# Layer 0's score rows in a four-layer graph network: broadcast transposes on TensorE, or one transpose and a trip through DRAM

## The chip, the cores and the metric

The kernel runs on one core of a Trainium2 chip. The metric is the device time of one execution in microseconds; lower is better. Five engines work side by side, each with its own queue of instructions: TensorE (PE) multiplies, VectorE (DVE) and ScalarE (ACT) do the elementwise work, GpSimd (POOL) does little here, and SyncE (SP) issues every DMA of the kernel's loop.

## The reference

32 graphs of 512 nodes with 256 features go through four layers. Each layer is followed by a residual sum and a layernorm. What matters here is layer 0, an attention with four heads of 64 features over the graph's edges:

```python
h = jnp.einsum('bnd,hde->bhne', nodes_embed, W)
e_src = jnp.einsum('bhne,hte->bhtn', h, a_src)
e_dst = jnp.einsum('bhne,hte->bhtn', h, a_dst)
...
    weight = weight + mask * (e_src[:, :, t, :, None] + e_dst[:, :, t, None, :])
weight = jax.nn.leaky_relu(weight, negative_slope=0.01)
weight = jnp.where(node_adj[:, None] == 0, NEG, weight)
attention = jax.nn.softmax(weight, axis=-1)
dst = jnp.einsum('bhij,bhje->bhie', attention, h) + bias[None, :, None, :]
out = jax.nn.relu(dst) + h
```

The score of an edge from i to j is a number of node i plus a number of node j. Layers 1 and 3 are attentions of the same kind with one head, layer 2 is a transformer block (eight heads and a feed forward).

## The kernel before

Each graph is held as four tiles of 128 nodes (R = 4) by 256 features (two halves, K = 2), all in float32. A matmul in float32 appears in the profile as two instructions; a transpose appears as one.

**Score rows.** The kernel lays the scores out with the key node j on the partitions and the query node i along the row. A leaky relu of a sum, exponentiated, is a maximum of products, so one VectorE instruction makes a tile of unnormalised attention: `kept` (line 393) takes `gb`, which is exp of the query's number, the same row of 512 on all 128 partitions, and `ex`, one number for each partition, and computes max(gb, ex) * edges. To get `gb`, `along` takes a column of 128 numbers for each node tile, repeats it 128 times, and transposes that on TensorE (four transposes of 128 by 128 into one PSUM bank, tile `gp`). ScalarE copies the bank to SBUF (line 345). Layer 0 calls `along` once for each of its four heads; layers 1 and 3 once each.

**Names.** h0p, h1p and h3p are the projections of layers 0, 1 and 3; o0, o1 and o3 here stand for their attention products, which the profile lists as `o<-hv,pt` (layer 0) and `o<-h,pt` (layers 1 and 3). hv is layer 0's value matrix. xt1p, xt2p, xt3p and ytp are transposes of a layer's input, ctp those of layer 2's context, qkp and vp the projections of layer 2, s its scores, cp its attention product, wop its output projection, f1p and f2p its feed forward.

**Order of work.** The function `graph` is a generator that does one small chunk of work at a time and then yields a key, `PERIOD * b + PLACES[name][i]`, where b is the graph. `heapq.merge` runs the chunks of all 32 graphs by their keys. PERIOD is 12054, and a graph's keys go from -1440 to 42379, so that some four graphs are under way at any time. In the TensorE queue the instructions stand in exactly this order (`manual_schedule`); in the other queues (DVE, ACT, POOL, SP) the framework orders them when the program is built, by what it estimates to be ready. [...]

**Buffers.** Tags are shared inside stages: layers 0 and 1 are stage a, layer 2's attention stage b, feed forward and layer 3 stage c. In stage a there are seven buffers of the tag `part`, which holds `kept`'s tiles, two for `gb`, and two PSUM banks. The adjacency halves (`adjt` for the mask at lines 363 and 371, `adj` for layer 2's symmetric mask at lines 384 to 387) all go through one buffer, so each load (line 351) waits in SP's queue until the half before it has been used up. Layer 2's scores of the last of four key tiles are masked by a matmul on TensorE in both kernels.

Of the kernel before, what the change touches and what calls it, by code (L numbers as in the profile page):

```python
# [9 lines left out]
F32 = mybir.dt.float32  # L10
# [10 lines left out]


F32R = mybir.dt.float32r
SHUT = -(2.0**127)


PERIOD = 12054
PLACES = {
    "edges": [-1440, -1440, -410, 1420],
    "x": [3260],  # L30
    "mask": [16220, 16520, 16600, 17520],
    "layer 0": [
        2410, 3594, 4534, 4534, 5073, 5753, 5753, 5823, 6123, 6123, 6233, 6233, 6603, 6773, 6903,
        7687, 7687, 7777, 8077, 8077, 8157, 8287, 8439, 8439,
    ],
    "layer 1": [11037, 11066, 11277, 11729, 11849, 11879, 12043, 13286, 13554, 14195, 14884],
    "qkv": [17180, 17740, 18270, 18270, 18270, 18990, 19484, 19654, 21635, 21635],
    "attention": [
        20262, 20932, 21922, 21982, 22092, 22092, 22092, 22350, 22350, 23077, 23537, 23537,
        24028, 24208, 24328, 24532, 25064, 25220, 25368, 25943,  # L40
    ],
    "projection": [26801, 26801, 26861, 26911, 27661, 27721, 28721, 29140, 29256, 29848],
    "feed forward": [
        31013, 31120, 32042, 32263, 32263, 32465, 32710, 33771, 33983, 34076, 34284, 34691,
        35070, 35329, 35615, 36103, 36646, 37299,
    ],
    "layer 3": [39714, 39714, 40906, 41226, 41406, 41526, 41526, 42359, 42359, 42379, 42379],
}
STAGES = {"edges": "a", "x": "a", "layer 0": "a", "layer 1": "a", "feed forward": "c", "layer 3": "c"}
ALL = mybir.DependencyInfo(mybir.DependencyClass.Sync, mybir.DependencyReason.DATA)  # L50
# [22 lines left out]
def fast_path(ctx: ExitStack, tc: tile.TileContext, a: dict, out: bass.AP, bad: bass.AP):  # L73
# [8 lines left out]
    nc = tc.nc  # L82
    B, N, D = a["x"].shape
    P = 128
    R = N // P
    K = D // P
    H, _, HO = a["w0"].shape
# [13 lines left out]
    def product(what, *args, **kwargs):  # L101
        latest[0] = what(*args, **kwargs).ins.name  # L102
# [19 lines left out]
    ident = const.tile([P, P], F32, name="ident")  # L122
# [24 lines left out]
    cols = const.tile([P, 5 * K + NF], F32, name="cols")  # L147
# [89 lines left out]

    sb = ctx.enter_context(tc.tile_pool(name="sb", bufs=1))  # L240
    ps = ctx.enter_context(tc.tile_pool(name="ps", bufs=2, space=bass.MemoryType.PSUM))
    stage = ["a"]

    def buf(shape, tag, name, bufs, dtype=F32):

        return sb.tile(shape, dtype, tag=tag + stage[0], name=name, bufs=bufs)

    def bank(name, dtype=F32):
        shape = [P, 2048 // (2 if dtype == BF16 else 4)]
        n = 4 if stage[0] == "b" else 2  # L250
        return ps.tile(shape, dtype, tag="mm" + stage[0], name=name, bufs=n)

    def part(name):

        return buf([P, N], "part", name, {"a": 7, "b": 6, "c": 5}[stage[0]])

    def all_rows(v):
        return v.unsqueeze(1).to_broadcast([P, R, D])

    def layernorm(y, eps):  # L260

        st = buf([P, R, 6], "bn", "bn", 2)
        mv = buf([P, R, 2], "mv", "mv", 2)
        rs = buf([P, 3, R], "rs", "rs", 2)
        for r in range(R):
            nc.vector.bn_stats(st[:, r, :], y[:, r, :])  # L266
            nc.vector.bn_aggr(mv[:, r, :], st[:, r, :])
        var = mv[:, :, 1]
        nc.vector.scalar_tensor_tensor(rs[:, 0, :], var, eps, var, op0=ALU.add, op1=ALU.max)  # L269
        nc.gpsimd.tensor_tensor(rs[:, 1, :], rs[:, 0, :], mhalf[:, :R], op=ALU.pow)  # L270
        nc.vector.scalar_tensor_tensor(  # L271
            rs[:, 2, :], mv[:, :, 0], -1.0, rs[:, 1, :], op0=ALU.mult, op1=ALU.mult
        )
        for r in range(R):
            nc.scalar.activation(  # L275
                y[:, r, :],
                y[:, r, :],
                AF.Identity,
                bias=rs[:, 2, r : r + 1],
                scale=rs[:, 1, r : r + 1],  # L280
            )
# [37 lines left out]
    def project(xt, w, cols, name):  # L319

        h = buf([P, R, cols], "h", name, {"a": 2}.get(stage[0], 1))
        for r in range(R):
            yield
            p = bank(name + "p")
            for k in range(K):
                product(nc.tensor.matmul,
                    p[:, :cols],
                    xt[:, k, r * P : (r + 1) * P],
                    w[:, k, :cols],
                    start=k == 0,  # L330
                    stop=k == K - 1,
                )
            nc.scalar.copy(h[:, r, :], p[:, :cols])
        return h

    def along(cols, name):

        yield
        p = bank("gp")
        for r in range(R):  # L340
            product(nc.tensor.transpose,
                    p[:, r * P : (r + 1) * P], cols[:, r, :].to_broadcast([P, P]), ident
            )
        g = buf([P, N], "gb", name, {"a": 2}.get(stage[0], 1))
        nc.scalar.copy(g, p)  # L345
        return g
# [27 lines left out]
    def symmetric(b, at):  # L374
# [4 lines left out]
        for h in range(2):  # L379
# [3 lines left out]
            for r in range(h * R // 2, (h + 1) * R // 2):  # L383
                in_place(nc.vector.tensor_max(parts[r], at[:, r, :], t[:, r % (R // 2), :]))
                diag = parts[r][:, r * P : (r + 1) * P]
                nc.vector.tensor_max(diag, diag, identb)
        nc.vector.tensor_scalar(shut, shut, 0.0, SHUT, op0=ALU.is_equal, op1=ALU.mult)
        return a2, shut

    def kept(name, g, edges, f):  # L390

        t = part(name)
        nc.vector.scalar_tensor_tensor(t, g, f, edges, op0=ALU.max, op1=ALU.mult)  # L393
        return t


    def layer0(x, xt, at, rd):
        h = yield from project(xt, w0, D + 2 * H, "h0")
        values = hv[:, :, :, :HO]
        nc.vector.tensor_add(  # L400
            values,
            h[:, :, :D].rearrange("p r (h e) -> p r h e", h=H),
            bias0.rearrange("p (h e) -> p h e", h=H).unsqueeze(1).to_broadcast([P, R, H, HO]),
        )
        ex = buf([P, 2, H, R], "ex", "ex0", 2)
        s, d = h[:, :, D : D + H], h[:, :, D + H :]
        nc.scalar.activation(ex[:, 0], s.rearrange("p r h -> p h r"), AF.Exp, scale=-0.99)
        nc.scalar.activation(ex[:, 1], d.rearrange("p r h -> p h r"), AF.Exp, scale=0.99)
        nc.scalar.activation(hv[:, :, :, HO], d, AF.Exp, scale=0.01)
        nc.vector.tensor_mul(values, values, hv[:, :, :, HO:].to_broadcast([P, R, H, HO]))  # L410
        y = sb.tile([P, R, D], F32, tag="y", name="y0", bufs=3)
        for hh in range(H):
            gb = yield from along(ex[:, 0, hh, :].unsqueeze(2), "gb0")
            pt = [kept("pt0", gb, at[:, j, :], ex[:, 1, hh, j : j + 1]) for j in range(R)]
            p = bank("o0")
            o = p[:, : R * HC].rearrange("p (r c) -> p r c", r=R)
            for r in range(R):
                yield
                for j in range(R):
                    product(nc.tensor.matmul,  # L420
                    o[:, r, :],
                        pt[j][:, r * P : (r + 1) * P],
                        hv[:, j, hh, :],
                        start=j == 0,
                        stop=j == R - 1,
                    )
            rdh = rd[:, hh * R : (hh + 1) * R].unsqueeze(2)
            nc.vector.reciprocal(rdh, o[:, :, HO:])  # L428
            nc.vector.scalar_tensor_tensor(
                y[:, :, hh * HO : (hh + 1) * HO],  # L430
                o[:, :, :HO],
                0.0,
                rdh.to_broadcast([P, R, HO]),
                op0=ALU.max,
                op1=ALU.mult,
            )
        nc.vector.tensor_add(x, x, all_rows(bet0))
        nc.vector.tensor_add(y, y, h[:, :, :D])
        head_layernorm(y, 1e-6)
        nc.vector.tensor_mul(y, y, all_rows(gam0))  # L440
        nc.vector.tensor_add(y, y, x)
        layernorm(y, 1e-5)
        return y
# [41 lines left out]
    def qkv(x):  # L485
        xt = yield from transposed([x[:, r, :] for r in range(R)], "xt2")
        qk = []
        for c in range(K):
            t = [sb.tile([P, 2, 2, N], F32R, tag="qk", name="qk", bufs=3) for _ in range(2)]
            for s in range(2):  # L490
# [10 lines left out]
                bias = bqk[:, s * K + c : s * K + c + 1]  # L501
                hi = sb.tile([P, N], F32R, tag="hi", name="hi", bufs=2)
                lo = sb.tile([P, N], F32R, tag="lo", name="lo", bufs=2)
                nc.scalar.activation(hi, p, AF.Identity, bias=bias)
# [155 lines left out]
    def layer3(x, at, rd):  # L660
# [16 lines left out]
        layernorm(x, 1e-5)  # L677
        return x

    ends = [0, R * H, R * (H + 1), R * (H + 1 + H2), ND]  # L680
    def load_x(b):
        xt = sb.tile([P, K, N], F32, tag="xt0", name="xt0", bufs=1)
# [63 lines left out]
            pass  # L746


    fine = sb.tile([P, 3], F32, name="fine")
    same = sb.tile([P, 2 * B], F32, name="same")  # L750
    nc.vector.tensor_tensor(same, sums[:, 0, :], sums[:, 1, :], op=ALU.is_equal)
    nc.vector.tensor_reduce(fine[:, 0:1], same, axis=X, op=ALU.min)
    nc.vector.tensor_reduce(fine[:, 1:2], ok, axis=X, op=ALU.min)
# [1 line left out]
    p = bank("badp")  # L755
# [645 lines left out]
```

## Time and profile before

| what | value |
|---|---|
| time, median of 3 runs | 3910.18 us (3910.09 to 3910.24) |
| the profiled execution's own time | 3906.41 us |
| span of its profile | 3904.6 us |
| PE busy | 3753.3 us (96% of the span) |
| DVE busy | 2674.8 us (69%) |
| ACT busy | 1926.2 us (49%) |
| DMA engines, mean busy share of queue 1 | 23.1% |

The profile's busy time of PE comes from pipelined matmuls whose ends are modelled, so that neighbouring matmuls overlap in it. What a matmul really takes from PE is read better as the distance from the start of one group in the timeline to the start of the next.

### The profile page before, as it was taken

How to read it: one execution, taken by the hardware profiler on the slowest of the kernel's cores; microseconds unless marked ns; L12 is line 12 of the kernel's file. 1: busy time of each engine (PE TensorE's matmuls, PEld its weight loads, DVE VectorE, ACT ScalarE, POOL GpSimd, SP SyncE). 2: the span in 40 equal slices, each digit the busy share in tenths (PEclk: the TensorE clock that was granted, in tenths of full speed). 3: DMA queues.
4: the chain of work that ended last, by engine and by line, in shares of the span. 5: the costliest groups of instructions: out<-in, count | busy, mean ns of one | idle time of the engine just before them, and what ended most of it. 6: DMA issues, size and time to landing. Idle time of an engine off the chain costs nothing.

```text
span 3904.6 us, 53602 instructions
## 1 busy us (share of the span) xinstructions
PE 3753.3 (96%) x19238; PEld 2824.5 (72%) x19238; DVE 2674.8 (69%) x5594; ACT 1926.2 (49%) x4257; POOL 346.9 (9%) x266
## 2 busy tenths in 40 slices
PE   5899999999999999999999999999999999999996
PEld 4577777777777777777777777777777777777764
DVE  4667676677677677677677677677777677777653
ACT  2444455444455544455544455545555544555442
POOL 0000010000010001010001010001010001010000
PEclk6899999999999999999999999999999999999998
DMA  3222222222222222222222222222222222221120
GB/s 106 77 73 65 72 58 67 71 76 67 70 60 65 71 76 69 68 62 63 71 76 71 66 63 64 69 76 71 66 65 65 65 76 74 63 67 58 49 54 12
DMA packets 180431, 261.20 MB, mean 67 GB/s; under 512 B 36800, under 2 KB 72768, under 8 KB 180160
## 3 DMA queue, kind: packets, MB, share of 16 engines
q1 hardware_dynamic: 180160, 257.71, 23.1%
q8 instruction: 155, 2.54, 0.3%
q14 instruction: 116, 0.95, 0.1%
HBM read 106.57 MB, written 16.78 MB: 32 GB/s over the span
## 4 chain that ended last, share of the span: by engine, by line
PE 60%; DVE 14%; issue 8%; ACT 5%; POOL 5%; POOLq 0%; ACTq 0%
PE o L102 16%; PE f1p L102 7%; PE f2p L102 6%; PE qkp L102 5%; PE cp L102 5%; DVE pr L556 4%; ACT y L275 4%; POOL rs L270 3%; PE h3p L102 3%; PE s L102 3%; PE h1p L102 3%; PE wop L102 3%; POOL st L297 2%; PE gp L102 2%; PE vp L102 2%
## 5 line engine op out<-in xcount | busy, mean ns | idle before, releaser
L556 DVE TENSOR_TENSOR pr<-pr,a 128x1024 f32<-128x1024 f32 x384 | 459.1, 1216 | 319.3 <-ACT pr L553 319.2
L275 ACT ACTIVATE y<-y,rs 128x256 f32<-128x256 f32 x768 | 398.4, 589 | 438.2 <-DVE rs L271 438.2
L393 DVE SCALAR_TENSOR_TENSOR pt<-gb,ex,at 128x512 f32<-128x512 f32 x768 | 530.6, 744 | 77.6 <-ACT gb L345 77.6
L553 ACT ACTIVATE pr<-s 128x512 f32<-128x512 f32 x1024 | 545.2, 613 | 7.4 <-PE s L102 7.3
L102 PEld LDWEIGHTS o<-hv,pt 128*128 128x128 f32 x4096 | 508.4, 199 | 23.7 <-issue 8.4
L102 PE MATMUL o<-hv,pt 128*128 128x65 f32 x4096 | 502.7, 280 | 9.7 <-DVE pt L393 9.7
L102 PE MATMUL f2p<-wf,ft 128*128 128x256 f32 x2048 | 491.6, 383 | 12.3 <-ACT ft L638 12.2
L102 PE MATMUL cp<-pr,v 128*64 128x512 f32 x2048 | 474.9, 600 | 17.8 <-DVE pr L556 17.1
L102 PE MATMUL f1p<-yt,wf 128*128 128x256 f32 x2048 | 488.9, 381 | 0.3 <-DVE yt L302 0.3
L102 PE MATMUL o<-h,pt 128*128 128x257 f32 x2048 | 482.8, 383 | 3.7 <-DVE pt L393 3.7
L102 PEld LDWEIGHTS o<-h,pt 128*128 128x128 f32 x2048 | 381.5, 190 | 96.0 <-issue 40.6
L270 POOL TENSOR_TENSOR rs<-rs,mhalf 128x4 f32<-128x4 f32 x192 | 246.2, 1282 | 2118.8 <-DVE rs L269 1826.0
L638 ACT ACTIVATE ft<-f1p,cols 128x256 f32<-128x256 f32 x512 | 215.2, 474 | 442.2 <-PE f1p L102 442.2
L102 PEld LDWEIGHTS f2p<-wf,ft 128*128 128x128 f32 x2048 | 380.1, 191 | 69.5 <-ACT ft L638 17.1
L102 PEld LDWEIGHTS f1p<-yt,wf 128*128 128x128 f32 x2048 | 385.3, 191 | 54.5 <-DVE yt L302 0.8
L102 PE MATMUL s<-qk 128*128 128x512 f32 x1024 | 395.1, 481 | 1.6 <-ACT pr L553 1.6
L102 PEld LDWEIGHTS cp<-pr,v 128*64 128x64 f32 x2048 | 133.0, 136 | 286.0 <-issue 194.2
L266 DVE BATCH_NORM_STATS2 bn<-y 128x6 f32<-128x256 f32 x768 | 294.6, 411 | 4.5
L102 PEld LDWEIGHTS s<-qk 128*128 128x128 f32 x1024 | 187.8, 190 | 99.3 <-issue 40.6
L102 PE MATMUL qkp<-xt,wqkv 128*128 128x512 f32 x512 | 231.3, 594 | 0.0
L345 ACT COPY gb<-gp 128x512 f32<-128x512 f32 x192 | 111.5, 581 | 219.4 <-PE gp L102 219.4
L428 DVE RECIPROCAL rd<-o 128x4 f32<-128x4 f32 x128 | 23.4, 183 | 272.7 <-PE o L102 272.7
(134 smaller groups left out, 4582.5 us busy)
## 6 DMA issues: line engine op xcount, KB each, us to landing
qk<-hi SPq DMA_DIRECT2D x1024, 64.0 KB, 2.0
qk<-lo SPq DMA_DIRECT2D x1024, 64.0 KB, 2.0
adjt<-in_adjt SPq DMA_DIRECT2D x64, 512.0 KB, 3.5
adj<-in_adj SPq DMA_DIRECT2D x64, 512.0 KB, 3.6
xt<-in_xt SPq DMA_DIRECT2D x32, 512.0 KB, 3.4
x<-in_x SPq DMA_DIRECT2D x32, 512.0 KB, 4.7
out<-y SPq DMA_DIRECT2D x32, 512.0 KB, 3.0
wf<-in_w1t SPq DMA_DIRECT2D x1, 1024.0 KB, 7.6
```

The source lines that it names most:

```text
L102: latest[0] = what(*args, **kwargs).ins.name
L266: nc.vector.bn_stats(st[:, r, :], y[:, r, :])
L270: nc.gpsimd.tensor_tensor(rs[:, 1, :], rs[:, 0, :], mhalf[:, :R], op=ALU.pow)
L275: nc.scalar.activation(y[:, r, :], y[:, r, :], AF.Identity, bias=rs[:, 2, r : r + 1], scale=rs[:, 1, r : r + 1],)
L297: nc.gpsimd.tensor_tensor(st[:, 2, :], st[:, 1, :], mhalf[:, :G], op=ALU.pow)
L345: nc.scalar.copy(g, p)
L393: nc.vector.scalar_tensor_tensor(t, g, f, edges, op0=ALU.max, op1=ALU.mult)
L428: nc.vector.reciprocal(rdh, o[:, :, HO:])
L553: nc.scalar.activation(t[:, i, :], s, AF.Exp, scale=QSCALE)
L556: nc.vector.tensor_mul(t, t, edges)
L638: nc.scalar.activation(ft[:, f, :], p[:, f, :], AF.Relu, bias=bf1[:, ff + f : ff + f + 1])
```

## The change

Layer 0 no longer calls `along`. After the two exponentials it transposes its sixteen columns (four heads by four node tiles) with one PE transpose, whose result is 16 rows of 128. ScalarE copies that to SBUF, a DMA writes it to an 8 KB tile in DRAM, and for each head another DMA reads that head's 512 numbers back onto all 128 partitions (256 KB written to SBUF). The rows of heads 0 and 1 are read at once, those of heads 2 and 3 after `kept` of heads 0 and 1. The exponential for hv and its product (lines 409 and 410) now stand after the DMAs' issue. `along` stays for layers 1 and 3. All keys in PLACES are new except for PERIOD, and two small tiles at the end of the program reuse buffers of `part`.

```diff
@@ (keys; "mask", "qkv", "attention", "projection", "feed forward" are new likewise)
-    "edges": [-1440, -1440, -410, 1420],
-    "x": [3260],
+    "edges": [-1240, -980, -470, 1660],
+    "x": [2610],
-    "mask": [16220, 16520, 16600, 17520],
+    "mask": [16880, 17050, 18310, 18310],
     "layer 0": [
-        2410, 3594, 4534, 4534, 5073, 5753, 5753, 5823, 6123, 6123, 6233, 6233, 6603, 6773, 6903,
-        7687, 7687, 7777, 8077, 8077, 8157, 8287, 8439, 8439,
+        3070, 4014, 4464, 4464, 5583, 5783, 5783, 6433, 6733, 6803, 6803, 6803, 6803, 7163, 7163,
+        7163, 7193, 9097, 9397, 9397, 9397, 9397, 9437, 9437, 9507,
     ],
-    "layer 1": [11037, 11066, 11277, 11729, 11849, 11879, 12043, 13286, 13554, 14195, 14884],
-    "qkv": [17180, 17740, 18270, 18270, 18270, 18990, 19484, 19654, 21635, 21635],
+    "layer 1": [11147, 11176, 12027, 12297, 12297, 12357, 12357, 13366, 13784, 13784, 15794],
+    "qkv": [17230, 17350, 18880, 19150, 19220, 19520, 20214, 20764, 21625, 21825],
...
-    "projection": [26801, 26801, 26861, 26911, 27661, 27721, 28721, 29140, 29256, 29848],
+    "projection": [25751, 26941, 27351, 27471, 27941, 28071, 28841, 29450, 29706, 30078],
...
-    "layer 3": [39714, 39714, 40906, 41226, 41406, 41526, 41526, 42359, 42359, 42379, 42379],
+    "layer 3": [40234, 40464, 41356, 41486, 41656, 41686, 41686, 42299, 42359, 42829, 43129],
@@
+    dram = ctx.enter_context(tc.tile_pool(name="dram", bufs=1, space=bass.MemoryType.DRAM))
@@ layer0
         nc.scalar.activation(ex[:, 1], d.rearrange("p r h -> p h r"), AF.Exp, scale=0.99)
+        rows = yield from rows_of(ex[:, 0].rearrange("p h r -> p (h r)"), "gr0")
+        gbs = []
+        for hh in range(2):
+            yield
+            gbs.append(over(rows, hh, "gb0"))
         nc.scalar.activation(hv[:, :, :, HO], d, AF.Exp, scale=0.01)
         nc.vector.tensor_mul(values, values, hv[:, :, :, HO:].to_broadcast([P, R, H, HO]))
         y = sb.tile([P, R, D], F32, tag="y", name="y0", bufs=3)
         for hh in range(H):
-            gb = yield from along(ex[:, 0, hh, :].unsqueeze(2), "gb0")
+            gb = gbs[hh]
             pt = [kept("pt0", gb, at[:, j, :], ex[:, 1, hh, j : j + 1]) for j in range(R)]
+            if hh + 2 < H:
+                yield
+                gbs.append(over(rows, hh + 2, "gb0"))
@@ new functions
+    def rows_of(cols, name):
+        m = cols.shape[1]
+        yield
+        p = bank("gp")
+        product(nc.tensor.transpose, p[:m, :P], cols, ident)
+        g = buf([m, P], "gr", name, 1)
+        nc.scalar.copy(g, p[:m, :P])
+        rows = dram.tile([m, P], F32, tag="rows", name=name + "d", bufs=2)
+        nc.sync.dma_start(rows, g)
+        return rows
+    def over(rows, i, name):
+        g = buf([P, N], "gb", name, 2)
+        src = rows[i * R : (i + 1) * R]
+        nc.sync.dma_start(g, bass.AP(tensor=src.tensor, offset=src.offset, ap=[[0, P], [1, N]]))
+        return g
@@ end of the program
-    fine = sb.tile([P, 3], F32, name="fine")
-    same = sb.tile([P, 2 * B], F32, name="same")
+    fine, same = part("fine")[:, :3], part("same")[:, : 2 * B]
```

More of the change, by code (lines that the diff above doesn't have):

```diff
@@ L28 @@
 PLACES = {
-    "edges": [-1440, -1440, -410, 1420],
-    "x": [3260],
-    "mask": [16220, 16520, 16600, 17520],
+    "edges": [-1240, -980, -470, 1660],
+    "x": [2610],
+    "mask": [16880, 17050, 18310, 18310],
     "layer 0": [
-        2410, 3594, 4534, 4534, 5073, 5753, 5753, 5823, 6123, 6123, 6233, 6233, 6603, 6773, 6903,
-        7687, 7687, 7777, 8077, 8077, 8157, 8287, 8439, 8439,
-    ],
-    "layer 1": [11037, 11066, 11277, 11729, 11849, 11879, 12043, 13286, 13554, 14195, 14884],
-    "qkv": [17180, 17740, 18270, 18270, 18270, 18990, 19484, 19654, 21635, 21635],
+        3070, 4014, 4464, 4464, 5583, 5783, 5783, 6433, 6733, 6803, 6803, 6803, 6803, 7163, 7163,
+        7163, 7193, 9097, 9397, 9397, 9397, 9397, 9437, 9437, 9507,
+    ],
+    "layer 1": [11147, 11176, 12027, 12297, 12297, 12357, 12357, 13366, 13784, 13784, 15794],
+    "qkv": [17230, 17350, 18880, 19150, 19220, 19520, 20214, 20764, 21625, 21825],
     "attention": [
-        20262, 20932, 21922, 21982, 22092, 22092, 22092, 22350, 22350, 23077, 23537, 23537,
-        24028, 24208, 24328, 24532, 25064, 25220, 25368, 25943,
+        20372, 21892, 22112, 22292, 22292, 22292, 22292, 22460, 22460, 23187, 23727, 23727,
+        24138, 24388, 24438, 25282, 25284, 25540, 25618, 26963,
     ],
-    "projection": [26801, 26801, 26861, 26911, 27661, 27721, 28721, 29140, 29256, 29848],
+    "projection": [25751, 26941, 27351, 27471, 27941, 28071, 28841, 29450, 29706, 30078],
     "feed forward": [
-        31013, 31120, 32042, 32263, 32263, 32465, 32710, 33771, 33983, 34076, 34284, 34691,
-        35070, 35329, 35615, 36103, 36646, 37299,
+        31123, 31230, 32013, 32313, 32393, 33195, 33320, 33881, 34093, 34186, 34364, 34741,
+        34820, 35365, 35395, 35883, 36226, 37209,
     ],
-    "layer 3": [39714, 39714, 40906, 41226, 41406, 41526, 41526, 42359, 42359, 42379, 42379],
+    "layer 3": [40234, 40464, 41356, 41486, 41656, 41686, 41686, 42299, 42359, 42829, 43129],
 }
```

## The prediction

> **What bounds the kernel now.** I read the page's busy times first, then one steady period in windows, then what PE waits for in it, and then the timeline of PE around layer 0. The page:
>
> ```profile
> PE 3753.3 (96%) x19238; PEld 2824.5 (72%) x19238; DVE 2674.8 (69%) x5594; ACT 1926.2 (49%) x4257; POOL 346.9 (9%) x266
> ```
>
> PE leads. The chain of work shows the same layernorm on POOL at 1898.55 and 2015.33 us, so a period (one graph in, one out) is 116.8 us. The window of that length gives busy PE, PEld, DVE, ACT, POOL, granted clock, DMA share and GB/s; PE's waits in the same window follow:
>
> ```profile
> 1898.55:2015.35 116.80, 115.11 (x602) 86.98 (x601) 83.09 (x174) 60.03 (x135) 10.78 (x9) 1.00 0.24 68
> ...
> PE gp L102 <- ACT ex L665: 0.7, 1, 0.7
> PE xt3p L102 <- ACT y L275: 0.5, 3, 0.2
> PE cp L102 <- DVE pr L556: 0.5, 1, 0.5
> ```
>
> PE is idle for 1.7 us of 116.8, in three places. The kernel is bound by PE's own work in its fixed order: what leaves PE is gained, and every microsecond for which PE waits at its next instruction is lost. Windows at 1000 and 3000 us give the same 115.11; 31 such periods are 3621 us, the rest (some 284 us) is filling and draining. Now the timeline of PE where layer 0 begins, and that of VectorE beside it (start, duration):
>
> ```profile
> 1960.22 0.60 PE L102 MATMUL gp<-ident,ex 128*128 128x128 f32 x4
> 1964.27 0.65 PE L102 MATMUL gp<-ident,ex 128*128 128x128 f32 x4 [0.70 <-ACT ex L665]
> 1966.50 3.68 PE L102 MATMUL o<-hv,pt 128*128 128x65 f32 x32
> 1970.02 0.60 PE L102 MATMUL gp<-ident,ex 128*128 128x128 f32 x4
> 1970.46 3.64 PE L102 MATMUL o<-h,pt 128*128 128x257 f32 x16
> ...
> 1963.23 2.72 DVE L393 SCALAR_TENSOR_TENSOR pt<-gb,ex,at 128x512 f32<-128x512 f32 x4
> 1967.34 2.73 DVE L393 SCALAR_TENSOR_TENSOR pt<-gb,ex,at 128x512 f32<-128x512 f32 x4
> ```
>
> Read: the transposes of head 0 start at 1960.22, its products 6.3 us later, without a wait; the group of layer 3 (1964.27) has 6.2 us until its products (1970.46). A group of four transposes takes 0.44 us from PE (1970.02 to 1970.46); starts likewise give 0.88 for one row tile of o0, 1.73 for one of o3, 0.865 for a wop chunk. The four tiles of `kept` take 2.7 us.
>
> **What the Trainium skill says.** "DMA: Bandwidth & Descriptors", section "Latency and other measured facts", puts the fixed cost of a DMA near 2 us, mostly the receipt from the target; the trace agrees (64 KB land after 2.0 us). Its section "Two DMAs through the same engine are not ordered" says that a DMA which reads what another wrote has to be held at the issuing engine until the first has completed: the two latencies add, and SP stands still in between. No DMA in this trace reads back what another wrote. The one read of exactly `over`'s form (2 KB onto 128 partitions) is in the trace three times; the row of the one that went alone at 48.55 us, and the usual small one:
>
> ```profile
> a<-in_a SPq DMA_DIRECT2D x1, 256.0 KB, 3.1
> ...
> qk<-hi SPq DMA_DIRECT2D x1024, 64.0 KB, 2.0
> ```
>
> Beside two half-megabyte loads it took 5.8 us.
>
> **The change part by part, for one period.**
>
> *Transposes.* Sixteen go (4 x 0.44 = 1.76 us of PE), one comes. It moves 128 columns through 16; a quarter of a group is 0.11, a lone transpose 0.27; I take 0.15. PE: **-1.61 us**. ACT loses four copies of 0.58 and gains one of about 0.3 (between 128x16 at 0.21 and 128x264 at 0.37); ACT is half idle, so that is worth nothing by itself.
>
> *The rows' way to VectorE.* Sorting the new keys (modulo 12054) gives PE's order: h3p, layer 3's `gp` (5524), the rows' transpose (5583), two wop, o3 tiles 0 and 1, eight xt2p transposes, o3 tile 2, then o0 of head 0 (6733). Between the rows' transpose and o0 lie 2 x 0.865 + 3 x 1.73 + 0.88 = 7.8 us. The chain beside it: transpose 0.3; ACT first copies layer 3's bank, 0.6, then the rows, 0.3; write to DRAM 2.0 (nearest row; 8 KB into DRAM is not in the trace, 1.5 to 3); read 3.1 (to 5.8); four `kept` 2.7: **9.0 us**. Tile 0 of o0 needs the last `kept` only for its last quarter, 0.66 us in, so 8.5 us are covered, and the stall at o3 (next) covers some more. On paper it just fits; but hv's product (1.2 us, now emitted after the DMAs), the second adjacency half (2 us) and o3's reciprocals (0.6 each) stand in VectorE's queue there, and a ScalarE layernorm block of 2.08 us can stand ahead of the rows' copy. I take **+1.0 us**; bounds 0 and 4.
>
> *Layer 3's products.* They lose the cover of head 0: in PE's order only the rows' transpose and two wop (2.3 us from the start of `gp`) remain ahead of them instead of 6.2. Chain, from the start of `gp`: ACT copy done at 1.3, VectorE's h times f (1.22) done at about 1.4, four `kept` until 4.1; the last is needed at 2.3 + 1.3 = 3.6. Stall 0.5; with one wop addition (0.42) or a layernorm statistic in between, more. I take **+0.8 us** (0.4 to 1.4).
>
> *Head 3 straight after head 2.* With seven buffers its fourth tile waits for head 2's last row tile; by the durations it just arrives. **+0.2 us** (0 to 0.8).
>
> *Layer 0's end.* Between the last o0 and layer 1's transposes PE had 27.1 us (2005.2 to 2032.3) and the layernorm was ready with 0.9 to spare. In the new order o0 ends later: 25.1 us of PE work, and half a microsecond of waiting if `cp` still waits, against a need of 26.2. **+0.7 us** (0 to 1.5).
>
> *xt3p.* From the last f2p to xt3p lie 17.8 us of PE work instead of 14.2; its stall of **0.5 us** goes.
>
> *DMAs.* Five more on SP per graph, 0.4 to 0.6 us each, 1 MB more traffic (DMA share 0.24, to about 0.27). The 64 qk issues occupy SP for some 40 us of each period, but their keys (from 6826) come after all five, so no cost there; if a row's read waits, they wait behind it, and their first user, s at 8318, is over 10 us of PE work later. `gb`'s two buffers: layer 3's is another tag, no conflict.
>
> Sum: -1.61 + 1.0 + 0.8 + 0.2 + 0.7 - 0.5 = **+0.6 us** per period, times 31 = +18. *Filling*: graph 0 pays the trip in a crowd of weight loads (some 12 us), but loses its three later gaps between `gp` and products (1.6 us each) and twelve transposes at half clock (1 us a group): about +4. Together +22 on the profiled execution's own 3906.4, which lies 3.8 below the median; on 3910.2 that is 3932; I round to **3930**.
>
> **Rivals.** *The trip is covered (faster).* All stalls at their lower bounds: -1.61 - 0.5 + 0 + 0.4 + 0 + 0.3 = -1.4 per period, -43: 3867. For it: o0 today waits for nothing, PE runs at 98.5%, and the chain is 9.0 against 8.5 plus the stall at o3. It decides when the rows are there by 6 us after their transpose. Against: VectorE has hardly a gap from 1950 to 1984 us.
>
> *SP's queue blocks.* Loads into the one adjacency buffer wait in SP's queue:
>
> ```profile
> SPq L351 <- DVE shut L386: 9.4, 1, 9.4
> ```
>
> Today nothing urgent stands behind. If the framework puts such a load ahead of the rows' DMAs, they come up to 9.4 us later, about 4 of which PE would see: +3.5 to +5 per period, some +130: 4040. The mask's keys (second half at 6256, after `over` 0 and 1) speak against it; SP's order isn't visible before the build. A hot read of one DRAM line, nearer 5.8 than 3.1, gives the same sign: +2.7, 4000.
>
> *It does nothing measurable.* Gain and stalls cancel: 3910. As the sum is +0.6 with 1.2 of uncertainty, this is a narrow band (0.2% is 8 us, about what a measurement of this kernel can tell from no change).
>
> **How the numbers follow.** Small loss (the forecast, 3918 to 3965): 0.38. Trip covered: 0.28. Cancelled: 0.14. Blocked or slow read: 0.20. That gives faster 0.28, same 0.14, slower 0.58; the likeliest case's own range is 3918 to 3965. Leaving out about one in ten at each end: 3858 to 4010.
>
> **What would show it.** Right: `gp` 256 instead of 768 plus 32 small ones; L345 64 copies; PE's work per period near 113.5; new waits of PE at o (both forms) for `pt`, and at xt1p for the layernorm, 2 to 3 us in all; none at xt3p. Wrong: no waits at o (the trip is covered, faster), or waits at o0 of several microseconds with SP standing at L351 just before the write (blocked), or `over` landing after 5 us.

## Result: 0.7 % slower, and the profile after

The changed kernel takes 3936.57 us (median of 4 runs, 3935.75 to 3936.82) against 3910.14 for the kernel before (median of 4, one more than in the table above; 3907.31 to 3910.24): ratio 1.0069, 95 % interval 1.0052 to 1.0086. That is a small loss, but clear of the spread between executions. The profiled execution took 3936.67 us, with a span of 3934.9. Lines were added above these places, so line 102 of the kernel before is now 103, 275 is 277, 345 is 347 and 393 is 395.

The page of the changed kernel, its busy times and the row of the new reads (KB of one, median us from issue to landing):

```profile
PE 3716.1 (94%) x18664; PEld 2758.6 (70%) x18758; DVE 2663.6 (68%) x5594; ACT 1888.3 (48%) x4161; POOL 399.6 (10%) x266
...
gb<-gr0d SPq DMA_DIRECT2D x128, 256.0 KB, 3.4
```

PE's records show 37 us less busy time than before (94 of this trace's 18758 matmul records are missing, so that the real difference may be smaller), and yet the span is 30.3 us longer. One period, from one layernorm on POOL to the next, in windows (busy time of PE, PEld, DVE, ACT and POOL, granted clock, DMA share, GB/s):

```profile
1914.48:2032.37 117.89, 114.17 (x585) 85.08 (x586) 82.65 (x175) 58.92 (x131) 12.54 (x9) 1.00 0.27 77
```

and what PE waited for in that window (us in total, times, longest):

```profile
PE f2p L103 <- ACT ft L648: 0.8, 1, 0.8
PE gp L103 <- ACT ex L675: 0.7, 1, 0.7
PE gp L103 <- ACT ex L474: 0.7, 1, 0.7
PE h3p L103 <- ACT h L335: 0.6, 1, 0.6
PE ctp L103 <- ACT cs L582: 0.5, 1, 0.5
PE ctp L103 <- DVE ctx L601: 0.2, 1, 0.2
PE xt1p L103 <- ACT y L277: 0.2, 1, 0.2
```

The period went from 116.80 to 117.89 us. PE's busy time fell by 0.94, but its idle time rose from 1.69 to 3.72. Of the seven waits only the second stood there before. None is at layer 0's products, where the rows arrive, and none names `pt` or a DMA. Five of the six new ones are on work of layers 1 and 2, layer 3's projection and the feed forward, which the trip does not touch.

The timeline where layer 0 begins, PE first, then ACT, DVE and SP (start, duration):

```profile
1980.04 0.76 PE L103 MATMUL gp<-ident,ex 128*128 128x128 f32 x5 [0.70 <-ACT ex L675]
1982.36 4.26 PE L103 MATMUL o<-h,pt 128*128 128x257 f32 x16
1986.46 1.04 PE L103 MATMUL xt2p<-ident,y 128*128 128x128 f32 x8
1987.33 1.90 PE L103 MATMUL o<-h,pt 128*128 128x257 f32 x8
1989.07 3.68 PE L103 MATMUL o<-hv,pt 128*128 128x65 f32 x32
1992.59 1.94 PE L103 MATMUL qkp<-xt,wqkv 128*128 128x512 f32 x4
...
1981.20 0.25 ACT L697 COPY gr<-gp 16x128 f32<-16x128 f32 x1
...
1981.40 2.73 DVE L395 SCALAR_TENSOR_TENSOR pt<-gb,ex,at 128x512 f32<-128x512 f32 x4
1986.02 2.73 DVE L395 SCALAR_TENSOR_TENSOR pt<-gb,ex,at 128x512 f32<-128x512 f32 x4
...
1981.48 0.33 SPq L699 DMA_DIRECT2D gr0d<-gr  x1
1982.85 6.25 SPq L706 DMA_DIRECT2D gb<-gr0d  x3
```

Follow the trip: the rows' transpose is the fifth instruction of the `gp` group at 1980.04 and starts at 1980.52; its copy on ACT ends at 1981.45, SP issues the write at 1981.48 and the first read at 1982.85, and that read lands at 1985.97. Head 0's four `kept` run from 1986.02 to 1988.75, and o0 starts at 1989.07 without a wait (from there to the next group are 3.52 us). The last `kept` is needed 0.66 us into o0, so the trip had about 1.0 us to spare. The DMA view of 1976 to 2000 us gives the write's landing:

```profile
gr0d<-gr SPq DMA_DIRECT2D x1, 8.0 KB, 1.4
```

Layer 3's products, ahead of it, show no wait either, but their first two row tiles took 4.10 us from PE (1982.36 to 1986.46) where two by the start-to-start time of the kernel before are 3.46: they run at the pace at which `kept` (1981.40 to 1984.13) delivers. This stall of 0.64 us counts as busy time.

### The profile page after: what moved, and what is told of

Read it like the earlier page. It is cut to its first block, busy times and chain, and to the rows that moved or that the text cites. A ratio compares the mean times of both kernels' runs of the same rounds, so it can differ in the third digit from the quotient of the medians.

```text
span 3934.9 us, 52538 instructions
## 1 busy us (share of the span) xinstructions
PE 3716.1 (94%) x18664; PEld 2758.6 (70%) x18758; DVE 2663.6 (68%) x5594; ACT 1888.3 (48%) x4161; POOL 399.6 (10%) x266
## 3 DMA queue, kind: packets, MB, share of 16 engines
q8 instruction: 151, 2.47, 0.3%
## 4 chain that ended last, share of the span: by engine, by line
PE 62%; DVE 16%; ACT 8%; POOL 5%; issue 1%; DMA 0%; POOLq 0%; ACTq 0%
PE o L103 16%; PE f2p L103 10%; PE f1p L103 10%; PE cp L103 6%; PE qkp L103 5%; ACT y L277 5%; POOL rs L272 5%; PE s L103 4%; DVE pr L566 3%; PE h1p L103 3%; DVE bn L268 2%; PE h3p L103 2%; PE vp L103 1%; PE wop L103 1%; PE gp L103 1%
## 5 line engine op out<-in xcount | busy, mean ns | idle before, releaser
L103 PEld LDWEIGHTS o<-hv,pt 128*128 128x128 f32 x4096 | 499.5, 198 | 41.4 <-issue 26.5
L103 PE MATMUL f2p<-wf,ft 128*128 128x256 f32 x2048 | 491.2, 383 | 30.4 <-ACT ft L648 30.3
L103 PE MATMUL o<-h,pt 128*128 128x257 f32 x2048 | 499.8, 387 | 3.4 <-DVE pt L395 3.1
L272 POOL TENSOR_TENSOR rs<-rs,mhalf 128x4 f32<-128x4 f32 x192 | 273.5, 1424 | 1952.1 <-DVE rs L271 651.1
L103 PE MATMUL qkp<-xt,wqkv 128*128 128x512 f32 x512 | 249.0, 610 | 0.9 <-ACT xt L306 0.9
L299 POOL TENSOR_TENSOR st<-st,mhalf 128x16 f32<-128x16 f32 x32 | 120.0, 3750 | 1052.3 <-DVE st L298 1052.3
L582 ACT COPY cs<-cp 128x512 f32<-128x512 f32 x128 | 74.0, 578 | 195.1 <-PE cp L103 195.1
```

The source lines that it names most:

```text
L299: nc.gpsimd.tensor_tensor(st[:, 2, :], st[:, 1, :], mhalf[:, :G], op=ALU.pow)
L582: nc.scalar.copy(t, cp)
```

## The experiments

The theory after these readings: **the trip is covered and worth about its 1.6 us; the loss comes from the new keys**, which set dependent chunks of PE work one behind the other. The rival: the trip itself costs the time (through DVE's and ACT's queues, SP, or the DMAs), and the waits follow from it.

### e1_order_only: the new keys without the trip

The rows are made by `along`, as before, at the places where the changed kernel issues its reads. Everything else, the keys too, is the changed kernel's.

```diff
-        rows = yield from rows_of(ex[:, 0].rearrange("p h r -> p (h r)"), "gr0")
+        yield
         for hh in range(2):
-            yield
-            gbs.append(over(rows, hh, "gb0"))
+            gbs.append((yield from along(ex[:, 0, hh, :].unsqueeze(2), "gb0")))
...
-                gbs.append(over(rows, hh + 2, "gb0"))
+                gbs.append((yield from along(ex[:, 0, hh + 2, :].unsqueeze(2), "gb0")))
```

> The changed kernel's keys and chunk order, but the rows come from four broadcast transposes per head on TensorE and a ScalarE copy, as before, at the places where the changed kernel issues its reads. Theory (the loss comes from the new order, which puts dependent pairs of chunks close together; the trip itself gains): the waits of PE at f2p, gp of layer 1, h3p and ctp stay (some 2.6 us per period) and the 1.6 us of transposes come back, so 117.9 + 1.6 = 119.5 us per period, about 3985 us (3970 to 3998). Rival (the trip through DRAM causes the loss, by its traffic, its place in SP's queue or the work it displaces): those waits go with the trip, period 116.8 or less, 3900 to 3940 us.

Measured: 3969.79 us, ratio to the kernel before 1.0156 (1.0139 to 1.0173). Its period in windows:

```profile
1923.27:2042.85 119.58, 115.19 (x601) 86.88 (x600) 82.53 (x175) 60.90 (x134) 11.27 (x8) 1.00 0.23 67
```

and PE's waits in that window:

```profile
PE o L103 <- DVE rs L271: 0.8, 1, 0.8
PE f2p L103 <- ACT ft L646: 0.8, 1, 0.8
PE gp L103 <- ACT ex L673: 0.7, 1, 0.7
PE gp L103 <- ACT ex L472: 0.7, 1, 0.7
PE h3p L103 <- ACT h L335: 0.6, 1, 0.6
PE ctp L103 <- ACT cs L580: 0.5, 1, 0.5
PE ctp L103 <- DVE ctx L599: 0.2, 1, 0.2
```

PE has the work of the kernel before (115.19 against 115.11), no row goes through DRAM, and still the waits at f2p, layer 1's `gp`, h3p and ctp stand there with the same lengths as in the changed kernel. The new keys alone cost 119.58 - 116.80 = 2.78 us a period, and the trip, laid on top of them, gains 119.58 - 117.89 = **1.69 us a period**: 1.02 of busy PE and the rest in waits, the one at o (0.8) above all. The rival falls. The 1.69 us hold for this order; in another the trip may meet other waits. In the whole run the trip gains less, 32.0 us of span instead of 31 x 1.69 = 52: the difference lies in the filling. From hv's product of the first graph (VectorE, line 417; 415 in e1) to that of the fourth, the changed kernel takes 308.2 us and e1 291.1. The layer 0 products of the first graph are part of it: in the changed kernel they begin at 29.14 us, after a wait of 10.99 for `pt`, and end at 58.2; in e1 they begin at 22.70 and end at 52.5. And 112.6 us of that stretch are at half clock, against 85.3 in e1, which by itself can make up to 14 of the 17 us.

### e5_second_hop: the trip made longer

The rows are copied once more, from DRAM to DRAM, before they are read back.

```diff
         nc.sync.dma_start(rows, g)
-        return rows
+        again = dram.tile([m, P], F32, tag="again", name=name + "e", bufs=2)
+        nc.sync.dma_start(again, rows)
+        return again
```

> The changed kernel with the rows copied once more, DRAM to DRAM, before they are read onto the partitions: the trip grows by one write's landing (1.4 us) and an issue (0.3 us), some 1.7 us. Theory (the trip is covered with about 1.0 us to spare before head 0's products): 0.7 us per period of new waits at o0, about 3958 us (3945 to 3975). Rival (the trip binds already): all of it shows, about 3990 us. Second rival (there is much more room than the trace suggests): 3937 us.

Measured: 4133.2 us, ratio 1.0573 (1.0556 to 1.0591), far above every expectation. The mechanism came as foreseen. PE's timeline where the rows are used:

```profile
1964.35 0.44 PE L103 MATMUL o<-hv,pt 128*128 128x65 f32 x2 [0.90 <-DVE pt L395]
1965.01 0.44 PE L103 MATMUL o<-hv,pt 128*128 128x65 f32 x2 [0.23 <-DVE pt L395]
...
1971.08 3.46 PE L103 MATMUL qkp<-xt,wqkv 128*128 128x512 f32 x4
```

The second hop landed after 1.8 us (DMA view), and o0 now waits 0.90 us and three times 0.23, 1.6 us in all. So the trip's length does reach PE once the spare microsecond is used up. The 1.6 us do not measure that spare time by themselves, since part of them is VectorE's order: head 0's row had landed at 1962.15, but the framework had put the mask's work ahead of the four `kept`, which follow it in VectorE's timeline at 1963.55 without a gap. And 1.6 us times 31 is only 50 us, where 197 were lost against the changed kernel. The rest shows in the last line: four qkp take 3.46 us where the changed kernel's take 1.94. The granted clock of PE fell to half (0.52 as the mean of 1967.00 to 1973.80 in windows; edges at 1967.3 and 1974.1), once in each period.

### e3_pairs_apart: dependent neighbours pulled apart, first attempt

Five keys of the changed kernel are moved (the expectation below says six) so that other PE work comes between cp and ctp, h1p and layer 1's `gp`, and the end of f1p and f2p.

```diff
     "layer 0": [
-        3070, 4014, 4464, 4464, 5583, 5783, 5783, 6433, 6733, 6803, 6803, 6803, 6803, 7163, 7163,
+        2858, 4014, 4464, 4464, 5583, 5783, 5783, 6433, 6733, 6803, 6803, 6803, 6803, 7163, 7163,
...
-    "layer 1": [11147, 11176, 12027, 12297, 12297, 12357, 12357, 13366, 13784, 13784, 15794],
+    "layer 1": [11147, 11176, 12027, 12297, 12297, 12357, 12395, 13600, 13784, 13784, 15794],
...
     "attention": [
-        20372, 21892, 22112, 22292, 22292, 22292, 22292, 22460, 22460, 23187, 23727, 23727,
+        20372, 21892, 22112, 22124, 22292, 22292, 22292, 22460, 22460, 23187, 23727, 23727,
...
-    "projection": [25751, 26941, 27351, 27471, 27941, 28071, 28841, 29450, 29706, 30078],
+    "projection": [26970, 26941, 27351, 27471, 27941, 28071, 28841, 29450, 29706, 30078],
```

> The changed kernel with six keys moved, so that other work lies between cp and ctp (h0p), between h1p and gp of layer 1 (cp), and between f1p and its f2p (the last s of head pair 0). Theory: the waits at ctp 0.53, gp of layer 1 0.70 and f2p 0.76 go, 2.0 us per period, 115.9 us, about 3875 us (3862 to 3895). Rival: the waits are set by displaced work and turn up at the next place, 3925 us or more.

Measured: 4090.04 us, ratio 1.0439 (1.0402 to 1.0475): a miss. The waits at f2p, layer 1's `gp` and ctp were gone, but layer 1's products now stood in a row. PE's timeline:

```profile
2027.69 3.64 PE L103 MATMUL o<-h,pt 128*128 128x257 f32 x16
2035.13 3.79 PE L103 MATMUL o<-h,pt 128*128 128x257 f32 x8 [3.80 <-ACT exp L487]
```

The third chunk waits 3.80 us; the profile names ACT's exponential at line 487 as its releaser, and in ACT's timeline the four instructions of a layernorm (line 277, 2.07 us from 2032.65) stand between that one and the step before it at line 486. The granted clock followed. Windows of 3.41 us, laid on the steps in which this record changes (PE busy first):

```profile
2030.18:2033.59 3.41, 1.15 (x6) 0.66 (x4) 1.49 (x5) 2.01 (x5) 1.01 (x1) 1.00 0.00 0
2033.59:2037.00 3.41, 1.87 (x4) 1.51 (x5) 2.21 (x2) 3.25 (x8) 0.00 (x0) 0.50 0.00 0
2037.01:2040.42 3.41, 3.41 (x9) 1.54 (x9) 3.41 (x15) 0.24 (x1) 0.00 (x0) 0.50 0.46 154
2040.42:2043.83 3.41, 3.41 (x17) 1.27 (x14) 0.71 (x5) 1.10 (x4) 1.01 (x1) 1.00 0.00 0
```

Here each step's clock goes with the step before it: 2.26 us idle, then half clock; 1.54 idle at half clock, half clock again; no idle, full clock.

### e7_pairs_apart_b: the same pairs, layer 1's products not in a row

```diff
-    "layer 1": [11147, 11176, 12027, 12297, 12297, 12357, 12395, 13600, 13784, 13784, 15794],
+    "layer 1": [11147, 11176, 12027, 12297, 12297, 12320, 12357, 13366, 13784, 13784, 15794],
```

(against the changed kernel's own line; the other three edits of e3_pairs_apart stay, so that four keys differ from the changed kernel, not five as the expectation says)

> The changed kernel with five keys moved: h0p between cp and ctp, the last s of head pair 2 (instead of a chunk of h1p) between h1p and gp of layer 1, the last s of head pair 0 between f1p and its f2p; layer 1's products stay at their keys. Theory: the waits at ctp 0.53 and 0.22, gp of layer 1 0.70 and f2p 0.76 go, a few tenths at xt1p are added, so 115.7 to 116.2 us per period, no stretch at half clock, about 3878 us (3862 to 3898). Rival (the waits are displaced work that turns up at the next place): 3920 us or more.

Measured: **3905.35 us** (median of 12 runs), ratio to the kernel before 0.9993 (0.9984 to 1.0002): the same as before, and 31 us less than the changed kernel. A period:

```profile
1898.64:2015.50 116.86, 114.36 (x587) 85.18 (x585) 82.78 (x175) 58.65 (x132) 11.32 (x9) 1.00 0.28 77
```

PE's waits in the window:

```profile
PE h3p L103 <- ACT h L335: 0.8, 1, 0.8
PE gp L103 <- ACT ex L675: 0.7, 1, 0.7
PE xt1p L103 <- ACT y L277: 0.5, 3, 0.2
PE ctp L103 <- DVE ctx L601: 0.2, 1, 0.2
PE h0p L103 <- ACT exp L487: 0.2, 1, 0.2
```

The waits at f2p (0.76), layer 1's `gp` (0.70) and ctp for `cs` (0.53) are gone, 2.0 us. About half of it came back: xt1p +0.33, h3p +0.18, h0p +0.18, and 0.19 more busy time. Net 117.89 - 116.86 = 1.03 us, times 31 = 32, as measured. This ties the loss to neighbouring dependent chunks by an edit and not by the trace alone. The expected 3878 was too low because it let only a few tenths of what was removed come back.

### e2 and e6: the trip in the old order

Two kernels lay the trip under the keys of the kernel before, with layer 0's own keys fitted to it (shown against the changed kernel's; all other keys are those of the kernel before). In the first one chunk of qkp is moved ahead (18270 to 18240), in the second it is left where it was.

```diff
     "layer 0": [
-        3070, 4014, 4464, 4464, 5583, 5783, 5783, 6433, 6733, 6803, 6803, 6803, 6803, 7163, 7163,
-        7163, 7193, 9097, 9397, 9397, 9397, 9397, 9437, 9437, 9507,
+        2410, 3594, 4534, 4534, 5073, 5073, 5073, 6190, 6199, 6199, 6199, 6199, 6199, 6233, 6233,
+        6603, 6773, 7687, 7687, 7777, 8077, 8157, 8287, 8439, 8439,
     ],
```

> The trip through DRAM under the old keys; only layer 0's own keys differ (the rows' transpose where head 0's group stood, head 0's products after the second row tile of layer 3's) and one qkp chunk moves ahead of layer 3's products as cover. Theory: the old waits (1.7 us per period) stay, 1.6 us of PE work go, a few tenths at o are added: 115.2 to 115.8 us per period, about 3870 us (3853 to 3888). Rival: the trip costs what the changed kernel lost, 3925 us or more.

> The trip under the old keys once more, now without moving a qkp chunk: only layer 0's own keys differ from the kernel before (rows' transpose where head 0's group stood, head 0's products after the second row tile of layer 3's). Theory (the trip gains 1.7 us of PE per period, the loss came from the new order elsewhere): the old waits of 1.7 us per period stay, 1.6 us of work go, some 0.7 us at layer 3's o and up to 0.5 at layer 0's are added, so 115.7 to 116.3 us per period, no stretch at half clock, about 3880 us (3862 to 3905). Rival (the trip costs more than it gains wherever it stands): 3925 us or more.

Measured: e2_trip_old_order 4107.72 us (1.0508, 1.0490 to 1.0525), e6_trip_old_order_b 4172.17 us (1.0659, 1.0639 to 1.0679). Both missed, by waits of several microseconds. In e2 the moved qkp waits 5.01 us for VectorE's copy of `xt` at line 304. In e6 there are two. The longer is at f2p, 3.8 us in each period: ScalarE first stands idle for a layernorm and works off its four instructions (line 277), and only then makes the second half of `ft`, whose input had been ready. The other is at layer 3's products; PE's timeline, and VectorE's beside it:

```profile
1971.83 0.64 PE L103 MATMUL o<-h,pt 128*128 128x257 f32 x2
1975.51 4.84 PE L103 MATMUL o<-h,pt 128*128 128x257 f32 x14 [3.04 <-DVE pt L395]
...
1970.97 0.74 DVE L395 SCALAR_TENSOR_TENSOR pt<-gb,ex,at 128x512 f32<-128x512 f32 x1
1972.05 4.73 DVE L395 SCALAR_TENSOR_TENSOR pt<-gb,ex,at 128x512 f32<-128x512 f32 x7 [0.34 <-DMA gb<-gr0d]
```

VectorE makes one `kept`, waits 0.34 us for the DMA that brings head 0's row, and makes seven more: the framework put head 0's four tiles into VectorE's queue ahead of layer 3's last three, and PE waits 3.04 us for layer 3's second. In both kernels half clock follows (6.8 us a period in e2). So these two say nothing on what the trip is worth in the old order; that stays open.

### e8_pairs_apart_c: the mask's second half ahead of layer 0

e7_pairs_apart_b with the last two keys of "mask" at 18104 instead of 18310.

> As e7, and the second half of the mask 206 keys earlier, so that the eight xt2p transposes (0.88 us) stand ahead of layer 3's first product as cover. If the cover works: 0.6 us per period less than e7, about 3860 us. If VectorE now does the mask's second half ahead of head 0's tiles: new waits at layer 0's o of about 1 us, 3900 us, or, if the wait brings half clock, over 4030 us.

Measured: 4152.08 us (1.0617, 1.0600 to 1.0635). Layer 3's third row tile waits in PE's timeline, and the next products run at half speed:

```profile
2096.80 3.76 PE L103 MATMUL o<-h,pt 128*128 128x257 f32 x8 [5.76 <-DVE y L684]
2100.35 6.93 PE L103 MATMUL o<-hv,pt 128*128 128x65 f32 x32
```

The products wait until VectorE's line 684 has read an earlier result and so frees its bank. That instruction stood in VectorE's queue behind head 0's `kept` and the mask's work. Moving the mask 206 keys ahead cost 247 us against e7.

### e9, e10 and e11: the waits that were left, one after the other

e9_xt1_later, against e7_pairs_apart_b:

```diff
-    "layer 1": [11147, 11176, 12027, 12297, 12297, 12320, 12357, 13366, 13784, 13784, 15794],
+    "layer 1": [11290, 11292, 12027, 12297, 12297, 12320, 12357, 13366, 13784, 13784, 15794],
```

e10_ln1_earlier, against e9_xt1_later:

```diff
     "layer 0": [
-        2858, 4014, 4464, 4464, 5583, 5783, 5783, 6433, 6733, 6803, 6803, 6803, 6803, 7163, 7163,
+        2858, 3400, 4464, 4464, 5583, 5783, 5783, 6433, 6733, 6803, 6803, 6803, 6803, 7163, 7163,
...
-    "layer 1": [11290, 11292, 12027, 12297, 12297, 12320, 12357, 13366, 13784, 13784, 15794],
+    "layer 1": [11290, 11292, 12027, 12297, 12297, 12320, 12357, 13366, 13784, 13784, 14914],
...
-    "layer 3": [40234, 40464, 41356, 41486, 41656, 41686, 41686, 42299, 42359, 42829, 43129],
+    "layer 3": [39662, 39762, 41356, 41486, 41656, 41686, 41686, 42299, 42359, 42829, 43129],
```

e11_wop_moved, against e10_ln1_earlier:

```diff
-    "projection": [26970, 26941, 27351, 27471, 27941, 28071, 28841, 29450, 29706, 30078],
+    "projection": [26970, 26941, 27351, 27471, 27941, 28071, 28841, 29648, 29706, 30078],
...
-    "layer 3": [39662, 39762, 41356, 41486, 41656, 41686, 41686, 42299, 42359, 42829, 43129],
+    "layer 3": [39662, 39762, 41356, 41486, 41656, 41686, 41720, 42299, 42359, 42829, 43129],
```

> As e7, with layer 1's two xt1p chunks behind the next f2p and f1p (3.5 us more cover for layer 0's closing layernorm). Theory (a wait goes when PE has other work at that place, and stays gone if nothing behind it depends on the moved chunk soon): the 0.5 us at xt1p go, some 116.4 us per period, about 3888 us (3878 to 3898). Rival (the chain is only shifted): 3905 us.

> As e9, and layer 1's last product ahead of the ctp group, so that layer 1's closing layernorm comes earlier and leaves ScalarE before layer 3's projection copies; one h0p and the xt3p chunks take its place as cover. Theory: the 0.8 us at h3p go too, 115.6 us per period, about 3863 us (3850 to 3885). Risk: xt3p now comes 2.5 us sooner after the feed forward and may wait 0.5 us, which gives back most of it.

> As e10, and one wop chunk between layer 3's last h3p and its gp group. Theory: the 0.7 us at gp of layer 3 go as well, 114.9 us per period, about 3840 us (3828 to 3870). Rival: the four h3p chunks now stand in a row and wait 0.9 us for their two PSUM banks, 3870 us.

Measured: 3960.45 us (1.0137, 1.0120 to 1.0154), 3987.96 (1.0199, 1.0182 to 1.0216) and 4085.18 (1.0450, 1.0433 to 1.0468). All missed upward, although the wait that each aimed at (xt1p, h3p, layer 3's `gp`) did go. In e9 a wait at f2p of 1.9 us took its place; e10 kept that, raised ctp's to 1.2 and added 0.5 at layer 3's products; e11 added 2.0 more there for line 684, had f2p's at 1.6, and h3p's 0.8 came back. The f2p wait of e9, ACT first: a layernorm's four instructions stand in its queue ahead of `ft`:

```profile
1938.53 2.07 ACT L277 ACTIVATE y<-y,rs 128x256 f32<-128x256 f32 x4 [5.03 <-DVE rs L273]
1940.51 0.81 ACT L648 ACTIVATE ft<-f1p,cols 128x256 f32<-128x256 f32 x2
1941.01 2.84 PE L103 MATMUL f2p<-wf,ft 128*128 128x256 f32 x8 [1.89 <-ACT ft L648]
```

Windows of e9 on the clock's steps:

```profile
1938.59:1942.00 3.41, 1.52 (x9) 0.89 (x6) 0.00 (x0) 3.41 (x7) 0.00 (x0) 1.00 0.08 19
1942.00:1945.41 3.41, 3.41 (x10) 2.65 (x9) 0.00 (x0) 0.83 (x3) 0.00 (x0) 0.50 0.56 154
1945.41:1948.82 3.41, 3.41 (x21) 3.00 (x20) 0.72 (x2) 2.36 (x6) 0.00 (x0) 1.00 0.43 153
```

The f2p wait leaves PE idle for 1.89 us of the first window, and the whole next window is at half clock: 10 matmuls instead of the 21 of the third. In this period e9 lost 119.30 - 116.86 = 2.44 us against e7. The trace itself splits that: in 20 periods one step is at half clock, in the others none, while the f2p wait is there in both. The first kind takes 119.3 us, the second 117.6. So a halved step costs 1.7 us, half its length, and the other 0.7 us are the longer waits (3.8 us against 2.4, with less busy time); e10 shows the same 1.7 (120.3 and 118.6). One further execution of each, of which no trace is kept, shows a mean clock of 0.981 and 0.983, as without halved steps, at an unchanged time (3960.98 and 3989.80 us); what took the time there is open.

## Why the prediction was right, and where its account was not

The forecast was a small loss, 3930 us, with 3918 to 3965 for that case; measured 3936.6. Its sum was +0.6 us a period, measured +1.09. The terms:

| step of the prediction | predicted, us a period | measured |
|---|---|---|
| transposes of layer 0 | -1.61 | -1.6: busy time -0.94, with the 0.6 of layer 3's stall (two rows below) taken off it |
| stall at o0 for the rows | +1.0 (0 to 4) | 0, about 1.0 to spare |
| stall at layer 3's products | +0.8 (0.4 to 1.4) | +0.6, within busy time |
| head 3 after head 2 | +0.2 (0 to 0.8) | 0 |
| layernorm ahead of xt1p | +0.7 (0 to 1.5) | +0.16 |
| xt3p | -0.5 | -0.5 |
| cp's wait for `pr` | left as it is | -0.5 |
| f2p, layer 1's `gp`, h3p, ctp | not seen | +0.76, +0.70, +0.65, +0.75 |

**Right.** PE as the bound; the size of the transposes; the xt3p wait's end; layer 3's stall, to 0.2 us; DMA share 0.27 as foreseen; SP did not block (its mask load stood at 1991.78, after the reads for heads 0 and 1). PE's busy time of 114.17 is the predicted 113.5 plus layer 3's hidden 0.6.

**The step that failed: the trip's chain at o0.** It set 9.0 us of chain against 8.5 of cover and charged +1.0 for a queue of work in VectorE ahead of `kept`. Measured from the rows' transpose (1980.52), the chain took 8.2 us (to 1988.75) and the cover was 9.2 (to 1989.73). The write was put at 2.0 and took 1.4; the read was put at 3.1 and took 3.1 here (3.4 as the median of the run, 3.0 to 7.3); and VectorE's work was placed so that `kept` started 0.05 us after the row had landed. "DMA: Bandwidth & Descriptors" of the Trainium skill, "Latency and other measured facts", names some 0.8 us as the least round trip through HBM; the 1.4 measured for 8 KB lies between that and the 2.0 of the nearest row, which was thus too dear a price. The rival "the trip is covered" was therefore right in its mechanism and wrong in its time: the gain was there (e1) and was spent elsewhere.

**What the prediction did not cost at all: the rest of the new order.** It read the new keys only around layer 0. The four new places cost 2.86 us a period. Three are pairs in which one PE chunk needs, through one ACT or VectorE instruction, what the chunk just ahead of it made: cp, `cs`, ctp; h1p, `ex`, `gp`; f1p, `ft`, f2p. The fourth is h3p, whose bank ACT's copy of the projection frees; here ACT works off a layernorm and layer 0's two exponentials (1974.70 to 1977.01) ahead of that copy. The three pairs can be found in the order of PE that the new keys give, and the profile of before has a price: the pair h3p, `ex`, `gp` of layer 3 showed a wait of 0.7. The two errors nearly cancel: 2.4 us too much (o0 1.0, xt1p 0.5, cp 0.5, head 3 and layer 3 0.2 each) against 2.9 left out. With 31 periods that is 15 us of net error in the steady part. The total came out right in part by luck; the account behind it was not. One sum of the prediction does not follow from its own terms: the rival "the trip is covered" takes every stall at its lower bound, but enters layer 0's end at +0.3, where the bound given is 0. With 0 that sum is -1.7 a period, and the rival's time 3857 us instead of 3867.

**Filling.** Predicted +4; the span grew by 30.3 and 31 x 1.09 is 33.8, so filling and draining gave 3.5 back. The long first wait of 10.99 us was in the prediction (12).

## What to carry to other kernels

When a change comes with a new order of work, price the order apart from the change: here one run with the old operations in the new order split +1.09 us into +2.78 and -1.69. On an engine that is 97 % busy, go through its whole new order and mark each chunk that needs, through another engine, what the chunk just before it made; each such pair cost 0.5 to 0.8 us here. Look at the other engine's queue as well: in e3, e6 and e9 the instruction that PE waited for stood right behind a layernorm in ScalarE's queue, in an order that the framework had chosen. A wait removed was worth half of its length in e7, since others grew behind it; and where one wait of PE grows to two microseconds, look at its clock before costing it at its length.

## What the hardware showed that was not expected

**Half clock after a wait of 2 us.** The granted clock changes in these traces only at multiples of 3.413 us. With windows laid on those steps over 300 to 3600 us of each trace, the idle time of PE in a step goes with the next step's clock:

| kernel | halved stretches in some 27 periods | PE idle in the step ahead: least, median, most | longest idle in the other full-clock steps |
|---|---|---|---|
| before | 0 | | 0.71 |
| the change | 0 | | 1.30 |
| e1_order_only | 0 | | 1.35 |
| e7_pairs_apart_b | 0 | | 1.40 |
| e9_xt1_later | 20 | 1.88, 1.89, 1.89 | 1.89 |
| e10_ln1_earlier | 13 | 1.88, 1.88, 1.89 | 1.88 |
| e11_wop_moved | 23 | 1.95, 1.99, 2.93 | 1.95 |
| e3_pairs_apart | 27 | 2.25, 2.26, 2.47 | 0.71 |
| e2_trip_old_order | 27 | 2.21, 2.29, 3.41 | 1.67 |
| e8_pairs_apart_c | 26 | 2.11, 3.41, 3.41 | 1.83 |
| e6_trip_old_order_b | 43 | 1.55, 2.73, 3.35 | 1.95 |
| e5_second_hop | 27 | 0.68, 1.35, 1.87 | 1.29 |

Every full-clock step with over 2.0 us of idle time was followed by half clock; between 1.5 and 1.95 it went both ways, and below 1.5 there was none but in e5. So the same wait costs more or less by where it falls in the steps: in e9 and e10 a wait of 1.9 us brought half clock, and with it 1.7 us more, only in some periods. The twelve kernels split by it: those without half clock stayed between 3905 and 3970 us, of those with it only e9 (3960) did, and the others took 3988 to 4172.

The Trainium skill's "TensorE: Matmul & The Clock Gate", Part 1, "What's actually happening", has the free-running window of 3413 ns and the two states, full and half clock, as here; it lets the clock fall after an idle window of some 3.4 us, where 2.0 of 3.41 were enough here, and the measurement decides. "A second HAM failure mode", in the same part, tells of many short idle times between groups of matmuls with the same effect, and e5's four short waits agree with it: 0.68 to 1.87 us of idle time in a step do there what 1.40 does not do in e7.

Idle time is not the whole of it: in e5, 39 steps at half clock with at most 0.19 us idle were followed by another at half clock. A count that fits better is how many columns the matmuls of a step stream, each weighted by the share of the array that it fills (cp's 128*64 counts half). With a line at 1580 columns a step, 16 of the 11602 steps of the twelve traces, at full and at half clock, fall on the wrong side, 13 of them in e6. In e5 the full-clock steps ahead of half clock streamed 539 to 1326 columns, the half-clock steps 924 to 1458 where half clock went on and 1613 or more where it ended; no step of the kernel before, the change, e1 or e7 streamed under 1810. This is read from the traces after the fact. No run changed that count alone, so it is not shown as the cause.

The change itself comes to 1.30 us of idle time in a step and the kernel before to 0.71, so that by this measure the change stands closer to half clock. Whether an order exists in which the trip beats the kernel before stays open: the best one found equals it.
